# A quarter of the state products of layer 0 on ScalarE and TensorE, with new PSUM turns and slots

## The chip, the core and the metric

The kernel runs on one core of a Trainium2 chip. The metric is the device time of one launch in microseconds. The core has five engines that run side by side, each in the order of its own queue: TensorE (PE), VectorE (DVE), ScalarE (ACT), GpSimd (POOL) and SyncE (SP), which here issues the DMA transfers. They wait for each other through semaphores.

## The reference, cut to what matters

The program is a network of four layers on a tensor of 4 x 96 x 64 x 64. Only layer 0 is touched by the change. It is two Mamba blocks, each over sequences of 4096 steps:

```
xc    = silu(causal_conv4(h @ in_w[:, :192]) + conv_b)          # [L, 192]
dbl   = xc @ xproj_w                                             # 6 + 16 (B) + 16 (C) columns
delta = softplus(dbl[:, :6] @ dt_w + dt_b)                       # [L, 192]
dA    = exp(delta[..., None] * A)                                # [L, 192, 16]
dBx   = delta[..., None] * B[:, None, :] * xc[..., None]         # [L, 192, 16]
state[t] = dA[t] * state[t - 1] + dBx[t]                         # the scan over L
y     = sum over the 16 states of state * C, + Dp * xc
out   = seq + (y * silu(z)) @ out_w
```

After the two blocks come a pooled branch, a fusing product and a batch norm. All of it is float32.

## The kernel before, in words

Layer 0 is cut into 32 items: 4 sequences x 4 stretches of T = 1024 steps x 2 blocks. Within an item the 192 x 16 = 3072 pairs of channel and state are 24 tiles of 128 partitions x 1024 steps. A tile is (p, g, j): p one of three groups of 64 channels, j a half of it (32 channels), g one of four groups of 4 states. So a partition of a tile is one state of one channel.

A tile needs `da` = exp(delta * A), by ACT (line 488); `u` = (delta * xc) * B; the scan, by DVE (line 529); then, for the two tiles of one (p, g) together, a product with C by POOL (line 534, `times_c`) and a sum over the states by PE into `y` (line 551, `sum_y`). `delta` and `du` = delta * xc come in a layout of 64 channels by 2 x 512 steps; they are stored to DRAM (line 383) and read back with every channel on four partitions (`ddb`, `udb`, line 430). B and C rows go to DRAM as `cd` and come back spread over the partitions (`brep`, `crep`, line 416).

The product with B is made in two ways. For 14 tiles PE spreads the rows of B into a PSUM buffer with a 0/1 matrix (`rep`, line 474, two matmuls), and DVE multiplies (line 523), in place or into a second PSUM buffer. For 10 tiles, those with g = 3 and four with g = 2, POOL multiplies from SBUF (lines 509 and 511, `times_b`), and `da` is then put into PSUM by ACT (`dap`). There are two PSUM buffers of 128 x 1024 for this, tags `x` and `u`: `rep` always takes `x`, `dap` and the out-of-place product always `u`. Two more banks hold the tiles of the first stage (`ps`), two hold `y`.

The order of the work is written by hand. A loop over m = 24 k + t (line 613) gives to each engine's queue, for tile t of item k: the scan, the next `rep` or `dap`, the exp of the tile three ahead, a one-element product that puts the incoming state into `da` (line 497, `enter`), then POOL's products, sums, gates and projections at listed slots. The first stage of an item (norm, convolution, xproj, delta, z) is cut into steps, each at a slot; a slot below zero lies in the item before the one before. The slot order is fixed for PE, DVE, ACT and POOL; an engine runs what stands in its queue strictly in that order. SP's order is left to the scheduler, which follows the order of the program.

The names that the prediction uses: `center` (line 282, norm by a matmul, waits for the load of `x`), `nt` transposes (318), `n` copies (329), xc convolution (215, 16 matmul records a part), `join` (229, xproj), `dbl` copies (369), delta parts, Softplus (377), Silu (350), `start_y` (544), `sum_y` (551), gate (562), project (569 and 229), finish (581 to 591). `prepare` makes the weights before the first item; its `conv_taps` is the table of convolution taps, loaded to 97 partitions.

Of the kernel before, what the change touches and what calls it, by code (L numbers as in the profile page):

```python
# [20 lines left out]
T = 1024  # L21
# [29 lines left out]
class Net:  # L51
# [43 lines left out]
    def layer0(self, dram, scratch):  # L95
        tc, nc, ins = self.tc, self.nc, self.ins
        x_in = ins["x"]
        with ExitStack() as ctx:
# [3 lines left out]
            psum_y = ctx.enter_context(tc.tile_pool(name="l0y", bufs=2, space=PSUM))  # L102
# [44 lines left out]
            AHEAD = 3  # L147

            weights = {}

            def load_weights():
                for name, shape in (
                    ("sel_r", [128, 32]),
                    ("sel_b", [64, 4, 128]),
                    ("xproj", [128, 3, 2, 3 * 2 * NST + DTR]),
                    ("out_w", [128, 3, C]),
                    ("fus", [C, 2, C]),
                    ("gpw", [C, C]),
                ):
                    weights[name] = load(cp, name, shape)  # L160
                nc.sync.dma_start(dtw[C:], ins["dtw"])

            def prepare():
                with tc.tile_pool(name="l0s", bufs=1) as wk, tc.tile_pool(name="l0g", bufs=1) as sums_pool:
                    in_w = load(wk, "in_w", [C, 2, HID])
                    rows = wk.tile([C + 1, 2, 4, DIN], F32, name="conv_taps")
                    nc.sync.dma_start(rows, ins["conv_rows"].partition_broadcast(C + 1))
# [5 lines left out]
                    nc.vector.tensor_scalar_mul(nega, nega, -1.0)  # L173

# [14 lines left out]

                    layer(0)  # L190

                    for m in sorted(stages[0])[:4]:
                        for f in stages[0].pop(m):
                            f()
                    layer(1)
# [12 lines left out]
            both = [(at, slice(64 * q, 64 * q + 64)) for q, at in enumerate(halves)]  # L208

# [51 lines left out]
            def first_stage(k):  # L261
# [16 lines left out]
                @at_slot(-9)  # L278
                def _():
                    m["ps"] = [tile_ps(128), tile_ps(128)]  # L280
                    for q in range(8):
                        nc.tensor.matmul(
                            m["ps"][q // 4][:, q % 4 * C : q % 4 * C + C],
                            m["xn"][:, q * 128 : q * 128 + 128],
                            self.center,
                            start=True,
                            stop=True,
                        )

                @at_slot(-8)  # L290
                def _():
                    if k:
                        nt = wk.tile([128, 2, T + 1], F32, name="nt", tag="up2")[:, 0]
                    else:
                        nt = first_pool.tile([128, 8 * C], F32, name="nt")
                    m["nt"] = nt[:, : 8 * C].rearrange("p (q c) -> p q c", q=8)
                    m["rs"] = cp.tile([128, 8], F32, name="rs", tag="rs")
                    for q in range(8):
                        nc.scalar.activation(
                            m["nt"][:, q],  # L300
                            m["ps"][q // 4][:, q % 4 * C : q % 4 * C + C],
                            AF.Square,
                            accum_out=m["rs"][:, q : q + 1],
                        )
                    nc.scalar.activation(m["rs"], m["rs"], AF.Ln, scale=1.0 / C, bias=self.eps)
                    nc.scalar.activation(m["rs"], m["rs"], AF.Exp, scale=-0.5)

                @at_slot(-7)
                def _():
                    for q in range(8):  # L310
                        x = m["ps"][q // 4][:, q % 4 * C : q % 4 * C + C]
                        nc.scalar.mul(m["nt"][:, q], x, m["rs"][:, q : q + 1])
# [9 lines left out]
                @at_slot(-5)  # L322
# [23 lines left out]
                parts_of("xc", [(w_x[:, i, k], k) for k in range(4)], n, ((-4, -2), (-3, 0), (-1, 1)), 2)  # L346

                @at_slot(2)
# [12 lines left out]
                @at_slot(4)  # L361
# [4 lines left out]
                @at_slot(5)  # L366
# [6 lines left out]
                parts_of("delta", [(dtw[:, i], 0)], dbl, ((6, 7), (6, 7), (7, 8)), 1)  # L373

                @at_slot(9)
                def _():
                    nc.scalar.activation(m["delta"], m["delta"], AF.Softplus)
                    exp_set()
# [6 lines left out]
                @at_slot(10)  # L385
# [3 lines left out]
                @at_slot(11)  # L389
# [7 lines left out]
                parts_of("z", [(w_z[:, i], 3)], n, ((12, 13), (12, 13), (13, 14)), 2)  # L397

                for p in range(3):
                    for j in range(2):  # L400
                        at_slot((15, 23, 31)[p] + j)(lambda p=p, j=j: load_d(m, p, j))
                    at_slot((16 if k else 15, 23, 31)[p])(lambda p=p: load_u(m, p))
                for g, t in ((0, 21), (1, 24), (3, 25), (2, 27)):
                    at_slot(t)(lambda g=g: load_c(m, g))
                at_slot(17 if k else 6)(lambda: load_b(m, 3))
                at_slot(22)(lambda: load_b(m, 2))
# [40 lines left out]
            outer = [(0, 0), (0, 1), (3, 0), (1, 0), (1, 1), (3, 1), (2, 0), (2, 1)]  # L447
            inner = [(0, 0), (3, 0), (0, 1), (3, 1), (1, 0), (2, 0), (1, 1), (2, 1)]
            order = [(p, g, j) for p, eight in enumerate((outer, inner, outer)) for g, j in eight]
            pool_tiles = (2, 5, 7, 9, 11, 13, 15, 18, 21, 23)  # L450
            group_starts = (0, 3, 6, 8, 10, 12, 14, 16, 19, 22)
            ends = {max(t for t, x in enumerate(order) if x[:2] == (p, g)): (p, g) for p in range(3) for g in range(4)}
            sums = {5: (0, 0), 8: (0, 1), 9: (0, 3), 12: (0, 2), 14: (1, 0), 16: (1, 3)}
            sums |= {18: (1, 1), 19: (1, 2), 23: (2, 0), 24: (2, 1), 26: (2, 3), 27: (2, 2)}
            starts = {3: 0, 13: 1, 17: 2}
# [3 lines left out]

            def on_pool(m):  # L460
                return m % NTL in pool_tiles
# [5 lines left out]
            def rep(m):  # L467

                k, t = divmod(m, NTL)
                x = psum_x.tile([128, T], F32, name="rep", tag="x")  # L470

                for q, at in enumerate(halves):
                    rows = slice(32 * q, 32 * q + 32)
                    nc.tensor.matmul(  # L474
                        x[:, at], sel_b[rows, order[t][1]], made[k]["dbl"][rows, at], start=True, stop=True
                    )
                return x

            def exp(m):
# [3 lines left out]
                if on_pool(m):  # L483
                    da = psum_x.tile([128, T], F32, name="dap", tag="u")
# [5 lines left out]
            def enter(m):  # L490

                k, t = divmod(m, NTL)
                b, s, i = items[k]
                col = column(t)
                if s:
                    a0 = made[k]["da", t][:, :1]
                    nc.scalar.mul(a0, a0, state[:, b, i, col : col + 1])

# [3 lines left out]
            def times_b(k, p, g, js):  # L502

                u = made[k]["ud", p]
                up = wk.tile([128, 2, T + 1], F32, name=f"up{g}", tag=f"up{g}", bufs=g - 1)[:, :, :T]
                for j in js:
                    made[k]["up", p, g, j] = up[:, j]
                if len(js) == 2:
                    nc.gpsimd.tensor_mul(up, u, twice(made[k]["brep", g]))  # L509
                else:  # L510
                    nc.gpsimd.tensor_mul(up[:, js[0]], u[:, js[0]], made[k]["brep", g])  # L511

            def scan(m, x):
# [4 lines left out]
                if on_pool(m):  # L518
                    u = made[k].pop(("up", h, g, j))
                else:  # L520

                    u = x if on_pool(m + 1) else psum_x.tile([128, T], F32, name="u", tag="u")
                    nc.vector.tensor_mul(u, made[k]["ud", h][:, j], x)  # L523
                if ("hs", h, g) not in made[k]:
                    made[k]["hs", h, g] = wk.tile([128, 2, T + 1], F32, name="hs", tag="hs", bufs=5)
                hs = made[k]["hs", h, g][:, j]
                col = column(t)
                st = 0.0 if s == 0 else state[:, b, i, col : col + 1] if on_pool(m) else 1.0
# [13 lines left out]
            def start_y(k, p):  # L542
                y = made[k]["y", p] = psum_y.tile([128, MB], F32, name="y", tag="y")
# [54 lines left out]
            b_slots = {3: [(0, 1, 3, (0, 1))], 4: [(0, 0, 2, (1,))], 9: [(0, 1, 2, (0, 1))], 13: [(0, 2, 3, (0, 1))]}  # L598
            b_slots[20] = [(0, 2, 2, (1,)), (1, 0, 3, (0, 1))]
# [10 lines left out]
            with tc.manual_schedule(engines=engines):  # L610
                gp = global_pool()
                first = min(stages[0])
                for m in range(first, last + 19):
                    k, t = divmod(m, NTL)
                    if 0 <= m < last:
                        scan(m, x)
                    if m == -14:
                        x = rep(0)
                    if 0 < m + 1 < last:
                        if on_pool(m + 1):  # L620
                            exp(m + 1)
                        elif (t + 1) % NTL in group_starts:
                            x = rep(m + 1)
                    if 0 <= m + AHEAD < last and not on_pool(m + AHEAD):
                        exp(m + AHEAD)
                    if 0 <= m + AHEAD - 1 < last and not on_pool(m + AHEAD - 1):
                        enter(m + AHEAD - 1)
# [4 lines left out]
                    for ahead, *what in b_slots.get(t, ()):  # L632
                        if 0 <= k + ahead < len(items):
                            times_b(k + ahead, *what)
                    for k0 in range(max(k - 1, 0), min(k + 1, len(items))):
# [13 lines left out]
                        if at == 35:  # L649
# [751 lines left out]
def _constants():  # L1401
# [3 lines left out]
    sel_b = np.stack([(k[:64, None] % 32 == 4 * g + p[None] // 32) for g in range(4)], 1)  # L1405
# [48 lines left out]
def _lay_out(i):  # L1454
# [20 lines left out]
    for k, v in (("rd", np.diagonal(a["r"])), ("id", np.diagonal(a["i"])), ("rb", a["rb"]), ("ib", a["ib"])):  # L1475
# [17 lines left out]
        "conv_rows": m["conv_w"].transpose(0, 2, 1)[None],  # L1493
# [39 lines left out]
```

## Time and profile before

| | |
|---|---|
| three timed runs | 3830.7, 3847.7, 3848.1 us, median 3847.7 |
| profiled execution, its own time | 3837.7 us |
| its span | 3835.5 us |
| layer 0's scans | from 78.9 to 2527.7 us |
| busy over the span | PE 3238.0, DVE 3036.5, POOL 2836.6, ACT 2387.5 us |
| granted PE clock, mean | 0.857 |

A row of the groups names the source line, the engine and the operation, what it writes and reads with partitions x elements, the count, the busy time and the mean of one in ns, and then the idle time of the engine just before it with what ended it. A fp32 matmul shows as two records. In the order of time the first two columns are the start and the length in us. A number in square brackets is the idle time before the instruction, with what ended it.

### The profile page before, as it was taken

The page shows a single profiled execution, that of the slowest core. Times are in us where ns is not written, and L with a number is a line of the kernel's source. Part 1 is how long each engine was busy: PE and PEld are TensorE (multiplying, and loading weights), DVE is VectorE, ACT ScalarE, POOL GpSimd, SP SyncE. Part 2 cuts the span into 40 slices and gives each one's busy share as a digit, 9 for nine tenths or more (in the row PEclk, how much of TensorE's full clock was granted, in tenths as well). Part 3 has the DMA queues.
Part 4 walks back from the last instruction along what each step waited for, and adds up shares of the span by engine and source line. Part 5 has one row for each costly group of instructions (what it writes and reads, how often), then busy time and mean ns, then how long its engine had stood idle before and what let it go on. Part 6 is the DMA issues. An engine that isn't in the chain of part 4 may idle for free. (4 is left out here: it accounts for less than half of the span.)

```text
span 3835.5 us, 43134 instructions
## 1 busy us (share of the span) xinstructions
PE 3238.0 (84%) x13656; PEld 1305.1 (34%) x13656; DVE 3036.5 (79%) x2704; ACT 2387.5 (62%) x4640; POOL 2836.6 (74%) x922
## 2 busy tenths in 40 slices
PE   6888888888888888888888888756799998999888
PEld 2222222222222222222222222126544534766643
DVE  4999999999999899999999999962573384444649
ACT  4666676666667666776666666541345686656557
POOL 1999999999999999999999999932001064444527
PEclk9888888887888778887878778757899999999989
DMA  7656666666676566666666666556200000011101
GB/s 182 167 154 165 165 165 165 165 161 154 165 172 164 145 165 163 160 157 165 157 154 169 161 158 163 151 135 211 77 1 1 1 1 6 18 37 35 36 9 58
DMA packets 177867, 463.82 MB, mean 121 GB/s; under 512 B 50804, under 2 KB 52734, under 8 KB 174304
## 3 DMA queue, kind: packets, MB, share of 16 engines
q1 hardware_dynamic: 177640, 461.08, 47.3%
q8 instruction: 108, 1.77, 0.2%
q14 instruction: 119, 0.97, 0.1%
HBM read 387.40 MB, written 73.50 MB: 120 GB/s over the span
## 5 line engine op out<-in xcount | busy, mean ns | idle before, releaser
L534 POOL TENSOR_TENSOR hs<-hs,crep 128x2048 f32<-128x2048 f32 x384 | 1595.8, 4186 | 30.8 <-DVE hs L529 27.0
L474 PE MATMUL rep<-dbl,sel_b 32*128 32x512 f32 x1280 | 458.7, 794 | 365.6 <-DVE hs L529 364.4
L529 DVE TENSOR_TENSOR_SCAN hs<-da,rep 128x1024 f32<-128x1024 f32 x320 | 732.1, 2288 | 35.1 <-ACT da L488 0.7
L488 ACT ACTIVATE dap<-ddb,nega 128x1024 f32<-128x1024 f32 x320 | 356.9, 1115 | 491.8 <-DVE hs L529 490.9
L509 POOL TENSOR_TENSOR up<-udb,brep 128x2048 f32<-128x2048 f32 x128 | 580.3, 4533 | 84.0 <-DMA ddb<-dd 82.8
L488 ACT ACTIVATE da<-ddb,nega 128x1024 f32<-128x1024 f32 x448 | 512.4, 1144 | 76.6 <-DVE hs L529 71.9
L529 DVE TENSOR_TENSOR_SCAN hs<-dap,state,up 128x1024 f32<-128x1024 f32 x240 | 558.1, 2325 | 0.0
L551 PE MATMUL y<-hs,sel_r 128*32 128x512 f32 x3072 | 522.5, 768 | 16.8 <-POOL hs L534 16.7
L523 DVE TENSOR_TENSOR rep<-udb,rep 128x1024 f32<-128x1024 f32 x320 | 388.5, 1214 | 71.2 <-PE rep L474 71.1
L215 PE MATMUL ps<-n,w_x 97*64 97x512 f32 x1536 | 367.2, 621 | 0.0
L474 PEld LDWEIGHTS rep<-dbl,sel_b 32*128 32x128 f32 x1280 | 120.5, 218 | 672.9 <-issue 547.4
L529 DVE TENSOR_TENSOR_SCAN hs<-da,u 128x1024 f32<-128x1024 f32 x128 | 293.0, 2289 | 12.6 <-DVE u L523 0.5
L1091 POOL CAST hq<-y 128x1536 fp8e5<-128x1536 f16 x64 | 93.9, 1467 | 218.8 <-issue 122.6
L215 PEld LDWEIGHTS ps<-n,w_x 97*64 97x64 f32 x1536 | 110.6, 141 | 254.8 <-issue 196.7
L551 PEld LDWEIGHTS y<-hs,sel_r 128*32 128x32 f32 x3072 | 71.9, 122 | 359.9 <-issue 266.9
L529 DVE TENSOR_TENSOR_SCAN hs<-dap,up 128x1024 f32<-128x1024 f32 x80 | 181.3, 2266 | 1.8 <-ACT dap L488 1.7
L523 DVE TENSOR_TENSOR u<-udb,rep 128x1024 f32<-128x1024 f32 x128 | 157.4, 1229 | 25.4 <-DMA udb<-ud 11.9
L965 POOL MEMSET h<- 1x4096 f32 x1 | 3.5, 3506 | 212.9 <-DVE n L871 212.9
L1230 POOL TENSOR_TENSOR av<-av,ec 128x780 f32<-128x780 f32 x32 | 58.7, 1836 | 133.7 <-ACT av L1227 133.7
L511 POOL TENSOR_TENSOR up<-udb,brep 128x1024 f32<-128x1024 f32 x64 | 151.6, 2369 | 0.0
L544 PE MATMUL y<-xc,dp 128*128 128x512 f32 x192 | 140.6, 821 | 0.0
L1203 POOL TENSOR_TENSOR f<-p,p 128x390 f32<-128x390 f32 x64 | 65.1, 1038 | 95.0 <-DVE p L1195 95.0
(260 smaller groups left out, 5962.0 us busy)
## 6 DMA issues: line engine op xcount, KB each, us to landing
ddb<-dd SPq DMA_DIRECT2D x768, 128.0 KB
udb<-ud SPq DMA_DIRECT2D x768, 128.0 KB
crep<-cd SPq DMA_DIRECT2D x512, 128.0 KB
brep<-cd SPq DMA_DIRECT2D x256, 128.0 KB
dd<-delta SPq DMA_DIRECT2D x64, 384.0 KB
band<-in_band SPq DMA_DIRECT2D x24, 1024.0 KB
ud<-delta SPq DMA_DIRECT2D x62, 384.0 KB
x<-in_x SPq DMA_DIRECT2D x32, 384.0 KB
```

What stands on the lines that cost most here:

```text
L215: nc.tensor.matmul(ps[rows], w[:, 64 * p : 64 * p + 64], rhs[:, at.start + shift : at.stop + shift], start=k == 0, stop=k == len(ws) - 1, ...
L474: nc.tensor.matmul(x[:, at], sel_b[rows, order[t][1]], made[k]["dbl"][rows, at], start=True, stop=True)
L488: nc.scalar.activation(da, made[k]["dd", h, j], AF.Exp, scale=nega[:, col : col + 1])
L509: nc.gpsimd.tensor_mul(up, u, twice(made[k]["brep", g]))
L511: nc.gpsimd.tensor_mul(up[:, js[0]], u[:, js[0]], made[k]["brep", g])
L523: nc.vector.tensor_mul(u, made[k]["ud", h][:, j], x)
L529: nc.vector.tensor_tensor_scan(hs[:, 1:], made[k].pop(("da", t)), u, st, ALU.mult, ALU.add)
L534: nc.gpsimd.tensor_mul(hs[:, :, :T], hs[:, :, 1:], twice(made[k]["crep", g]))
L544: nc.tensor.matmul(y, dp[:, items[k][2], p], made[k]["xc"][:, p], start=True, stop=True)
L551: nc.tensor.matmul(made[k]["y", p][row : row + 32], sel_r, made[k]["hs", p, g][:, j, at], start=False, stop=True, skip_group_check=True,)
L1091: nc.gpsimd.tensor_copy(q, y2, saturate=False)
L1203: nc.gpsimd.tensor_add(f[i][:, r], pp[0][:, :, r, :], pp[1][:, :, 1 - r, :])
```

## The change

g = 3 becomes the ScalarE group (`GA`), g = 2 the POOL group (`GP`), g = 0 and 1 stay with DVE: 6, 6 and 12 tiles of an item.

For the ScalarE group the product is made with time on the partitions. PE transposes `dbl`'s 32 rows of B and C (8 transposes) into a `y` bank, and ACT keeps four columns of it as `bt`. PE transposes `du` (three parts, 4 transposes each) into a `y` bank, and ACT copies each to `udt`. ACT then writes `uta`, 32 instructions of 128 x 192 elements, each with one column of `bt` as its scale, over nine slots. When the tile comes, PE transposes 8 blocks of `uta` back into the PSUM buffer from which the scan reads `u`.

The two PSUM buffers now alternate by tile (`banks`), and the fills are listed by slot (`fills`). The tiles have a new order in each third. POOL makes six single products. The scan takes the incoming state as its pointer operand in every tile; `enter` is gone. `hs` has four named buffers in place of a ring of five, `nt` a buffer of its own, `y` two tags. Nearly all steps of the first stage, loads and sums have new slots. In `prepare` the convolution taps are loaded as one row and spread to 97 partitions by PE (three matmuls with K = 1) and DVE copies, in place of a broadcast DMA of 582 KB.

```diff
+            GP, GA = 2, 3
-                    ("sel_b", [64, 4, 128]),
+                    ("sel_b", [64, 2, 128]),
-                    rows = wk.tile([C + 1, 2, 4, DIN], F32, name="conv_taps")
-                    nc.sync.dma_start(rows, ins["conv_rows"].partition_broadcast(C + 1))
+                    row = load(wk, "conv_rows", [1, 2 * 4 * DIN])
...
+                    def spread_taps(q):
+                        at = slice(q * MB, (q + 1) * MB)
+                        ps = wide(C + 1, MB, q)
+                        nc.tensor.matmul(ps, one, row[:, at], start=True, stop=True)
+                        nc.vector.tensor_copy(taps[:, at], ps)
...
+            def y_bank(k):
+                return psum_y.tile([128, MB], F32, name="y", tag=f"y{k % 2}")
...
...
-                        nt = wk.tile([128, 2, T + 1], F32, name="nt", tag="up2")[:, 0]
+                        nt = wk.tile([128, 8 * C], F32, name="nt", tag="nt")
-                parts_of("xc", [(w_x[:, i, k], k) for k in range(4)], n, ((-4, -2), (-3, 0), (-1, 1)), 2)
+                parts_of("xc", [(w_x[:, i, k], k) for k in range(4)], n, ((-5, -4), (-3, -2), (-2, -1)), 2)
...
-                parts_of("delta", [(dtw[:, i], 0)], dbl, ((6, 7), (6, 7), (7, 8)), 1)
+                parts_of("delta", [(dtw[:, i], 0)], dbl, ((4, 4), (4, 4), (5, 5)), 1)
...
+                @at_slot(8)
+                def _():
+                    m["tb"] = y_bank(3 * k - 2)[:, : 8 * 2 * NST].rearrange("p (q s) -> p q s", q=8)
+                    for q in range(8):
+                        nc.tensor.transpose(
+                            m["tb"][:, q], dbl[: 2 * NST, q * 128 : q * 128 + 128], self.ident[: 2 * NST, : 2 * NST]
+                        )
+
+                @at_slot(9)
+                def _():
+                    m["bt"] = cp.tile([128, 8, 4], F32, name="bt", tag="bt", bufs=2)
+                    nc.scalar.copy(m["bt"], m["tb"][:, :, 4 * GA : 4 * GA + 4])
-                parts_of("z", [(w_z[:, i], 3)], n, ((12, 13), (12, 13), (13, 14)), 2)
+                parts_of("z", [(w_z[:, i], 3)], n, ((12, 12), (12, 12), (13, 13)), 2)
+                def turn_du(p):
+                    ps = m["ut", p] = y_bank(3 * k - 3)
+                    for a in range(4):
+                        at = slice(a * 128, a * 128 + 128)
+                        nc.tensor.transpose(ps[:, at], m["du"][:, p, at], self.ident)
+
+                def keep_du(p):
+                    if p == 0:
+                        m["udt"] = m["delta"].rearrange("t p (q c) -> t p q c", q=8)
+                    nc.scalar.copy(
+                        m["udt"][:, p].rearrange("t (h a) c -> t a h c", h=2),
+                        m.pop(("ut", p)).rearrange("t (a h c) -> t a h c", a=4, h=2),
+                    )
+
+                for p in range(3):
+                    at_slot(14 + p)(lambda p=p: (turn_du(p), keep_du(p)))
+
+                def weigh(of):
+                    if of[0] == 0:
+                        m["uta"] = wk.tile([128, 8, 6, 128], F32, name="uta", tag="uta")
+                    for e in of:
+                        q, s4 = divmod(e, 4)
+                        nc.scalar.mul(
+                            m["uta"][:, q, :, 32 * s4 : 32 * s4 + 32].rearrange("t (p j) d -> t p j d", p=3),
+                            m["udt"][:, :, q].rearrange("t p (j d) -> t p j d", j=2),
+                            m["bt"][:, q, s4 : s4 + 1],
+                        )
+
+                e = 0
+                for t, count in ((19, 4), (20, 3), (21, 4), (22, 3), (24, 3), (25, 4), (26, 2), (27, 3), (28, 6)):
+                    at_slot(t)(lambda of=range(e, e + count): weigh(of))
+                    e += count
...
+            d0, d1 = [(0, 0), (0, 1)], [(1, 0), (1, 1)]
+            p0, p1, a0, a1 = ([(g, j)] for g in (GP, GA) for j in range(2))
+            thirds = d0 + p0 + d1 + p1 + a0 + a1, d0 + p0 + a0 + d1 + p1 + a1, a0 + a1 + d0 + p0 + d1 + p1
+            order = [(p, g, j) for p, third in enumerate(thirds) for g, j in third]
+            fills = {2: 3, 5: 6, 6: 7, 7: 8, 10: 11, 11: 12, 14: 15, 15: 16, 16: 17, 17: 18, 20: 21, 23: 24}
...
+                if g == GA:
+                    for q in range(8):
+                        nc.tensor.transpose(x[:, q * 128 : q * 128 + 128], made[k]["uta"][:, q, 2 * h + j], self.ident)
+                    return
...
-                if len(js) == 2:
-                    nc.gpsimd.tensor_mul(up, u, twice(made[k]["brep", g]))
-                else:
-                    nc.gpsimd.tensor_mul(up[:, js[0]], u[:, js[0]], made[k]["brep", g])
+                up = made[k]["up", p, j] = wk.tile([128, T], F32, name="up", tag=f"up{j}")
+                nc.gpsimd.tensor_mul(up, made[k]["ud", p][:, j], made[k]["brep", GP])
...
-                st = 0.0 if s == 0 else state[:, b, i, col : col + 1] if on_pool(m) else 1.0
+                st = state[:, b, i, col : col + 1] if s else 0.0
...
+            b_slots = {1: (0, 0, 1), 3: (0, 1, 0), 9: (0, 1, 1), 11: (0, 2, 0), 20: (0, 2, 1), 23: (1, 0, 0)}
```

Steps of which only the slot number changes, left out above: `center` from -9 to -11, Square -8 to -10, `nt` products -7 to -9, `n` copies -5 to -6, Silu 2 to -1, the xproj join 4 to 3, `dbl` copies 5 to 3, Softplus 9 to 6, the store of `delta` 10 to 7, `du` and its store 11 to 9, `finish` 35 to 34. The load of `x` stays at -14.

## The prediction

> **What bounds the kernel now.** I first read the busy time by stretch, over layer 0 (75 to 2530 us; the rest of the kernel is not touched).
>
> ```profile
> core 0: us, PE busy (x) PEld busy (x) DVE busy (x) ACT busy (x) POOL busy (x), PEclk, DMA share, GB/s
> 75.00:2530.00 2455.00, 2067.51 (x8359) 597.67 (x8357) 2315.92 (x1312) 1624.06 (x3004) 2413.83 (x607) 0.82 0.64 159
> ```
>
> POOL is busy 98%, DVE 94%. The scans start at 78.9 us and the last ends at 2527.7: 32 items of 76.5 us. Next, the groups by form:
>
> ```profile
> L534 POOL TENSOR_TENSOR hs<-hs,crep 128x2048 f32<-128x2048 f32 x384 | 1595.8, 4186 | 30.8 <-DVE hs L529 27.0 <-PE y L551 3.7
> L529 DVE TENSOR_TENSOR_SCAN hs<-da,rep 128x1024 f32<-128x1024 f32 x320 | 732.1, 2288 | 35.1 <-ACT da L488 0.7 <-ACT dap L488 0.5 <-DVE rep L523 0.5
> L509 POOL TENSOR_TENSOR up<-udb,brep 128x2048 f32<-128x2048 f32 x128 | 580.3, 4533 | 84.0 <-DMA ddb<-dd 82.8 <-DMA crep<-cd 1.3
> L529 DVE TENSOR_TENSOR_SCAN hs<-dap,state,up 128x1024 f32<-128x1024 f32 x240 | 558.1, 2325 | 0.0
> ...
> L523 DVE TENSOR_TENSOR rep<-udb,rep 128x1024 f32<-128x1024 f32 x320 | 388.5, 1214 | 71.2 <-PE rep L474 71.1
> ...
> L394 POOL TENSOR_TENSOR delta<-delta,xc 128x1536 f32<-128x1536 f32 x31 | 106.7, 3441 | 0.0
> ...
> L312 ACT ACTIVATE nt<-ps,rs 128x96 f32<-128x96 f32 x248 | 60.3, 345 | 0.0
> ```
>
> Divided over an item, POOL has 12 x 4.186 + 4 x 4.533 + 2 x 2.369 (L511) + 3.441 = 76.5 us: exactly the period. POOL is the bound. The DVE pitches are in the order of time:
>
> ```profile
> 1424.79 2.33 DVE L529 TENSOR_TENSOR_SCAN hs<-dap,state,up 128x1024 f32<-128x1024 f32 x1
> 1427.20 1.23 DVE L523 TENSOR_TENSOR u<-udb,rep 128x1024 f32<-128x1024 f32 x1
> 1428.54 2.29 DVE L529 TENSOR_TENSOR_SCAN hs<-da,u 128x1024 f32<-128x1024 f32 x1
> 1430.74 1.21 DVE L523 TENSOR_TENSOR rep<-udb,rep 128x1024 f32<-128x1024 f32 x1
> 1432.05 2.29 DVE L529 TENSOR_TENSOR_SCAN hs<-da,rep 128x1024 f32<-128x1024 f32 x1
> ```
>
> A DVE tile takes 1.33 + 2.21 = 3.54 us, a POOL tile 2.24, or 2.42 where a product into a fresh buffer follows; a gate adds 0.58. 14 x 3.54 + 10 x 2.24 + 4 x 0.18 + 3 x 0.58 = 74.4 us, so DVE has 2.1 us to spare per item. Last, the waits of layer 0 and PE's order of time:
>
> ```profile
> ACT dap L488 <- DVE hs L529: 490.9, 205, 4.8
> PE rep L474 <- DVE hs L529: 364.4, 180, 6.3
> ```
>
> ```profile
> 1425.02 2.08 PE L474 MATMUL rep<-dbl,sel_b 32*128 32x512 f32 x4 [2.16 <-DVE hs L529]
> ...
> 1443.88 1.13 PE L474 MATMUL rep<-dbl,sel_b 32*128 32x512 f32 x4 [1.24 <-DVE hs L529]
> ```
>
> ACT and PE wait 15 and 11 us per item for a PSUM buffer: that is their reserve. The fill that follows a long wait takes 2.08 us, the other 1.13.
>
> [...]
>
> **The change, part by part, per item.**
> *POOL*: two B rows become one; 10 tiles' products become 6 single ones. 50.2 + 6 x 2.369 + 3.4 = 67.9 us: 8.6 less, no longer the bound.
> *DVE*: 12 own tiles, 6 POOL tiles, 6 ScalarE tiles. The state is now a pointer in every scan with s > 0. By form the same scan takes 2.325 with it and 2.266 without, so +0.06 on three quarters of the 12 DVE tiles' scans, 0.5 us; the 2.24 of the others holds it already. 12 x 3.54 + 12 x 2.24 + 6 x 0.18 + 1.74 + 0.5 = 72.7 us (the 0.18 falls before each of six pairs), 72.8 with `da` in SBUF for six of them (2.288 against 2.266). This is the new floor, 3.7 below the period.
> *ACT*: off, 14 one-element products on 3/4 of the items, 0.19 pitch: 2.0. On, 32 weighings of 192 elements: 0.19 + 0.16 = 0.35 each, 11.2 (bounds 0.32, L312's rate, and 0.45 with L312's unoverlapped 0.345: 10 to 14); three copies of `du` at 0.58, 1.7; `bt` 0.2. 417.8 us per 610 (the stretch from 690) is 52.4; it becomes 63.5. It fits in 73, but only in queue order.
> *PE*: off, 10 fills of 1.06 pitch; on, 6 of them, 48 transposes of `uta`, 12 of `du`, 8 of `dbl`. L318 gives 0.13 a transpose with 96 weights, L834 (128x128) 0.147: 7.1 + 1.7 + 0.8. Sum +5.4; 64.7 busy (515.5 us per 610) become 70.
> *Moved*: all first-stage steps 1 to 4 slots. Products into `delta` go from slot 11 to 9, so their two stores of 384 KB now stand ahead of the next `x` load in SP's queue, with the store of `xd` too; `center`, which needs that `x`, moves from slot 15 to 13. `hs` has four named buffers for five in a ring, `nt` one of its own.
> *Prologue*: DVE waits 23 us for `conv_taps` until 29.9 us. Three K=1 matmuls replace that load: some 15 us earlier at the first convolution. But in item 0 the weighings and the next item's convolutions and Silu now stand ahead of its second exp group on ACT, roughly 12 us. I count zero, bounds -12 to +8.
>
> **Where DVE will still wait**, from full-clock pitches (sum_y 0.99, xc 3.58, join 2.76, start_y 1.06, a ScalarE tile's fill 1.2):
> 1. From the fill at slot 17, PE has two sum_y, start_y and a third sum_y, transposes, then (after ACT's 1.2 us copies to `n`) xc, fill, sum_y, xc, sum_y, xc: some 20.1 us. Behind the last, ACT has copy 0.55, Silu and table loads 5.5, exp 1.05, three weighings 1.05, exp of the POOL tile 1.1: 9.3. Both, and scans 2 to 16 (43.6), make 73.0 plus handoffs: as long as DVE's floor itself. I take 0.7 lost before scan 2.
> 2. PE idles about 4 us in slots 0 to 2, so the fill, sum_y and part of join in slots 2 to 4 run at half clock; copies of `dbl`, next exp and the six last weighings follow. Join so ends some 2.5 us later; the six weighings end 0.6 late for the tile at slot 6.
> 3. `x`: `du` ends on POOL 18.5 us after scan 4 (three C products, one B, `du`); 1.57 MB at the 240 GB/s of a `ud` store (3.3 us of packets), plus 1.7 to start: 8.2. `center` 1.95 and the tile 15 fill 1.2 end at 29.9 of the 29.5 to 30 that DVE needs: 0.3. All fills of 15 to 18 queue behind `center`.
> 4. Turning `du` in slots 15 and 16 waits for ACT's copies of the one before (ACT has Square and `nt` work between); the fill of 18 stands behind it: 0.3.
> Sum 1.9, so 74.7 us per item: (76.5 - 74.7) x 32 = 58 us off. The profiled execution's own time is 3837.7 (span 3835.5): 3780. The three timed runs are 3831 to 3848, median 3848, 10 above it; I leave the level at the profile's, 3780.
>
> **Rivals.**
> *PE and ACT become the bound* (slower). 70 us of PE work, 4 idle in slots 0 to 2, 1 to 2 waiting for `x`, is already 75.5. If half clock holds where it now recovers, say through the transposes of slots 14 to 17 (three fills 0.9 longer each, fill of 18 0.85, center 1.7) and slots 5 to 7 (two more fills), DVE waits 6 rather than 1.9: 79 us, +80, 3918. It decides once the waits exceed 3.7 us per item. For it: the half clock in a third of layer 0, in-order queues. [...]
> *POOL's relief is eaten* (no change). Only `x` has to be 1.7 us later than worked out: 76.5 us, 3838.
> *Nearly the floor*. The new slots hide items 1 to 4: 73.3, 103 us off, 3735.
> That the change is inert is excluded: POOL's instruction count falls.
>
> **How the numbers follow.** Forecast 0.48 (own range 3755 to 3815), floor 0.14, no change 0.12, slower 0.26. A measurement of this kernel tells about 0.5% from nothing, 19 us: faster 0.62, same 0.12, slower 0.26. The range: the low end is the floor; the high end holds half of the slower case (78 us per item): 3735 to 3885. ACT's 0.45 bound (+3 us in ACT's chain) lies inside it.
>
> **What would show it.** POOL's busy share in layer 0 falls to about 90%, DVE's rises to 97%; 12 single B products less double ones per item; weighings at 0.35 pitch; waits of DVE on the fills below 2 us per item, found at tiles 2, 6, 15 and 18. Wrong if DVE waits above 3.7 us per item on the `uta` fills or on ACT's exp, if PE's clock drops below 0.8, or if ACT's weighings cost over 0.45.

## The result, and the profile after

The changed kernel takes 3934.6 us (median of four runs, 3931.4 to 3935.7), the kernel before 3845.6 us in the same comparison (3830.7 to 3848.1). The ratio is 1.024, with a 95% interval of 1.021 to 1.027. The change made the kernel slower by 89 us, where 58 us faster were forecast.

The profiled execution has a span of 3933.9 us, 98.4 more than before. The loss lies in layer 0, whose scans now run from 68.5 to 2628.6 us:

| | before | after | difference |
|---|---|---|---|
| first scan starts | 78.9 | 68.5 | -10.4 |
| item 0 | 76.8 | 85.6 | +8.9 |
| items 1 to 31, each | 76.52 | 79.82 | +3.30, together +102.4 |
| last scan ends | 2527.7 | 2628.6 | +100.9 |

First the busy time over layer 0, in the columns of the same view of before.

```profile
core 0: us, PE busy (x) PEld busy (x) DVE busy (x) ACT busy (x) POOL busy (x), PEclk, DMA share, GB/s
75.00:2620.00 2545.00, 2017.70 (x9936) 788.52 (x9932) 2255.13 (x1240) 1947.02 (x3793) 2131.56 (x603) 0.87 0.58 146
```

POOL has gone from 98% to 84%, DVE from 94% to 89%, ACT from 66% to 77%. No engine is full any more: POOL stopped being the bound, and nothing took its place as a busy engine. So the new time is made of waits. The mean clock granted to TensorE in layer 0 rose, from 0.82 to 0.87, so the average hides what is found below about single places. The groups by form of the changed kernel (instructions with the same line, tiles and shapes together), with the rows that answer to those of before and those of the new operations:

```profile
L600 POOL TENSOR_TENSOR hs<-hs,crep 128x2048 f32<-128x2048 f32 x384 | 1598.4, 4178 | 415.3 <-DVE hs L595 297.8
L595 DVE TENSOR_TENSOR_SCAN hs<-da,state,rep 128x1024 f32<-128x1024 f32 x288 | 669.6, 2340 | 116.7 <-PE rep L544 103.7
...
L571 POOL TENSOR_TENSOR up<-udb,brep 128x1024 f32<-128x1024 f32 x192 | 452.9, 2359 | 68.6 <-DMA udb<-ud 59.7
...
L451 ACT ACTIVATE uta<-delta,bt 128x192 f32<-128x192 f32 x1024 | 380.9, 443 | 0.0
...
L595 DVE TENSOR_TENSOR_SCAN hs<-da,rep 128x1024 f32<-128x1024 f32 x96 | 217.7, 2281 | 43.3 <-PE rep L544 39.8
```

The prices are near the forecast: six single B products of 2.359 us per item, the weighings (L451) at 0.443 us by the record of one and 0.37 of ScalarE's time for each (380.9 us for 1024, where 0.35 was forecast; an estimate from the pitches of the kernel before, 0.19 for one element and 1.05 for 1024, also gives 0.35 for 192), and a scan with the state as a pointer at 2.340 against 2.281 without, the +0.06 of the working. The last columns are what changed. POOL used to stand idle 31 us ahead of its C products, and now stands idle 415, most of it for the scans. The scans wait for `rep` filled at line 544, which is TensorE turning `uta` back into the scan's buffer. The waits of layer 0 say the same, and go one step further back (waited time in total, times, longest):

```profile
DVE hs L595 <- PE rep L544: 143.5, 56, 6.3
...
PE ps L299 <- DMA x<-xd: 58.5, 15, 4.4
PE ps L299 <- DMA x<-in_x: 50.9, 13, 4.9
```

In 28 of 31 items `center` (now line 299) waits for the load of `x`, 3.9 us each time: 109 us together. No such wait stood in the kernel before, where `center` comes two slots later and `x` stands ahead of the stores of `du` in SP's queue. Two lines of SP's queue before, 13 us apart:

```profile
1407.00 1.30 SPq L258 DMA_DIRECT2D x<-in_x  x1
...
1420.09 1.24 SPq L383 DMA_DIRECT2D ud<-delta  x2
```

To place the loss inside the item I took the distance from each scan's start to the next one's, by position in the item, as a mean over items 2 to 30, and set against it what the instructions between them take (2.26 for a bare scan, 3.54 with a DVE product, 0.58 more for a gate). The sum of the differences is 7.2 us, which with the floor of 72.8 gives the 80.0 of an item:

| scan waits before | predicted, us per item | measured |
|---|---|---|
| tile 15 (fill behind `center`, behind `x`) | 0.3 | 4.4 |
| tile 2 (exp behind the Silus) | 0.7 | 1.2 |
| tile 21 | none | 0.9 |
| tile 18 (turning of `du`) | 0.3 | 0.3 |
| tile 6 (weighings) | 0.6 | 0.25 |

One item in the order of time, changed kernel, start and length in us: the end of `du` on POOL, then SP's queue, then TensorE, then the scans on DVE.

```profile
1390.53 3.44 POOL L424 TENSOR_TENSOR delta<-delta,xc 128x1536 f32<-128x1536 f32 x1
```

```profile
1394.00 1.24 SPq L413 DMA_DIRECT2D ud<-delta  x2
1395.33 1.29 SPq L661 DMA_DIRECT2D scratch<-x  x1
1396.72 1.95 SPq L275 DMA_DIRECT2D x<-in_x  x1
1398.72 1.68 SPq L492 DMA_DIRECT2D ddb<-dd  x3
```

```profile
1404.12 3.69 PE L299 MATMUL ps<-center,x 96*128 96x96 f32 x16 [3.88 <-DMA x<-in_x]
1407.60 1.91 PE L544 MATMUL rep<-ident,uta 128*128 128x128 f32 x8
```

```profile
1402.49 2.34 DVE L595 TENSOR_TENSOR_SCAN hs<-dap,state,up 128x1024 f32<-128x1024 f32 x1
1409.55 6.82 DVE L595 TENSOR_TENSOR_SCAN hs<-da,state,rep 128x1024 f32<-128x1024 f32 x3 [4.72 <-PE rep L544]
```

`du` ends at 1393.97. SP can then issue two stores of `du` and one of the block's output, and only at 1396.72 the load of `x`, for which `center` waits until 1404.12, 10.1 us after `du` (10.3 on the mean over 29 items). TensorE has stood still for 3.9 us by then, and does `center` and the fill for tile 15 at half the clock: 3.69 us (3.48 to the start of the fill) and 1.91, where the experiments below show 1.9 to 2.0 and 1.04. The scan of tile 15 starts 4.7 us late, and everything after it in the item is late with it. The busy time by stretch, in the columns from above, has the granted clock of TensorE from 1404 to 1408 us at 0.52:

```profile
1394.00:1404.10 10.10, 5.61 (x30) 1.14 (x23) 9.83 (x7) 6.34 (x10) 8.38 (x3) 1.00 0.87 212
1404.00:1408.00 4.00, 3.88 (x18) 3.91 (x19) 0.83 (x1) 0.00 (x0) 4.00 (x2) 0.52 1.00 239
```

The trace shows both halves of this. The load of `x` is used 7.4 us after its issue at 1396.72, and the two stores of `du` move ahead of it: their 384 packets of 2 KB (786 KB) start from 1395.23 us on, 98% of them by 1398.87, and packets of 4 KB, among which those of `x` are, start from 1398.31 on. The wait for `x` is 3.9 us on the mean, and the half clock follows: in the 27 items with a wait of 3.2 to 4.9 us `center` took 2.9 to 3.7 us and the fill after it 1.85 to 1.92. But it followed shorter waits too: in two items of this kernel TensorE waited 1.63 and 1.24 us ahead of `center`, and the fill behind it still took 1.91; in the kernel before, the fill that the prediction shows at 2.08 us had waited 2.16. So the length of one wait does not decide it here, and the last section has what the traces show in its place.

### The profile page after: what moved, and what is told of

Its sections match the earlier page's. It is cut to its first block, busy times and chain, and to the rows that moved or that the text cites. A ratio compares the mean times of both kernels' runs of the same rounds, so it can differ in the third digit from the quotient of the medians.

```text
span 3933.9 us, 46826 instructions
## 1 busy us (share of the span) xinstructions
PE 3209.7 (82%) x15326; PEld 1508.4 (38%) x15326; DVE 2993.5 (76%) x2644; ACT 2722.3 (69%) x5456; POOL 2567.5 (65%) x922
## 5 line engine op out<-in xcount | busy, mean ns | idle before, releaser
L595 DVE TENSOR_TENSOR_SCAN hs<-da,state,rep 128x1024 f32<-128x1024 f32 x288 | 669.6, 2340 | 116.7 <-PE rep L544 103.7
L571 POOL TENSOR_TENSOR up<-udb,brep 128x1024 f32<-128x1024 f32 x192 | 452.9, 2359 | 68.6 <-DMA udb<-ud 59.7
L549 PE MATMUL rep<-dbl,sel_b 32*128 32x512 f32 x768 | 252.7, 737 | 168.5 <-DVE hs L595 167.8
L451 ACT ACTIVATE uta<-delta,bt 128x192 f32<-128x192 f32 x1024 | 380.9, 443 | 0.0
L595 DVE TENSOR_TENSOR_SCAN hs<-dap,state,up 128x1024 f32<-128x1024 f32 x144 | 335.9, 2332 | 27.7 <-ACT dap L560 23.7
L595 DVE TENSOR_TENSOR_SCAN hs<-da,state,u 128x1024 f32<-128x1024 f32 x144 | 338.1, 2348 | 18.9 <-PE y L617 3.6
L544 PE MATMUL rep<-ident,uta 128*128 128x128 f32 x1536 | 257.4, 318 | 80.4 <-DVE hs L595 63.0
L544 PEld LDWEIGHTS rep<-ident,uta 128*128 128x128 f32 x1536 | 212.6, 167 | 176.7 <-issue 102.4
L595 DVE TENSOR_TENSOR_SCAN hs<-da,rep 128x1024 f32<-128x1024 f32 x96 | 217.7, 2281 | 43.3 <-PE rep L544 39.8
L586 DVE TENSOR_TENSOR rep<-udb,rep 128x1024 f32<-128x1024 f32 x192 | 232.3, 1210 | 0.0
```

What stands on the lines that cost most here:

```text
L451: nc.scalar.mul(m["uta"][:, q, :, 32 * s4 : 32 * s4 + 32].rearrange("t (p j) d -> t p j d", p=3), m["udt"][:, :, q].rearrange("t p (j d) - ...
L544: nc.tensor.transpose(x[:, q * 128 : q * 128 + 128], made[k]["uta"][:, q, 2 * h + j], self.ident)
L549: nc.tensor.matmul(x[:, at], sel_b[rows, g], made[k]["dbl"][rows, at], start=True, stop=True)
L571: nc.gpsimd.tensor_mul(up, made[k]["ud", p][:, j], made[k]["brep", GP])
L595: nc.vector.tensor_tensor_scan(hs[:, 1:], made[k].pop(("da", t)), u, st, ALU.mult, ALU.add)
```

## The experiments

My theory after this comparison: the late load of `x` and the half clock that follows its wait are the whole of the slowdown, and ScalarE's added work is not. The rival is the one that the prediction names: TensorE and ScalarE as a chain are the bound, so that a wait taken away at tile 15 comes back elsewhere.

### The load of `x` two slots earlier

```diff
-                @at_slot(-14)
+                @at_slot(-16)
                 def _():
                     m["xn"] = load_x(b, s, i) if k else x0
```

> The changed kernel with one edit: the load of x of the item after next is issued at slot 8 in place of slot 10, so that it stands ahead of the two stores of du and of the store of xd or scratch in SP's queue. Theory A (the load of x behind those stores holds center, center holds the fill of tile 15 in PE's queue, and DVE stands there 4.4 us an item): the wait before the scan of tile 15 falls from 4.4 to about 0.3 us, PE does center at full clock (1.95 in place of 3.5 us), the item goes from 80.0 to about 75.8 us, and the kernel from 3934 to about 3800. Theory B (PE and ACT are full, whatever x does): the wait moves to the tiles behind (18, 21 and 2), the item stays above 78.5 us, and the kernel above 3885.

Measured: 3781.6 us (3781.3 to 3785.0), ratio to before 0.986 (0.983 to 0.989). One number in the source takes some 150 us off the changed kernel and makes it faster than the one before. Items take 75.05 us. SP's queue, TensorE and DVE in this kernel, at the same place in the item:

```profile
1378.53 0.42 SPq L275 DMA_DIRECT2D x<-in_x  x1
1382.28 1.24 SPq L413 DMA_DIRECT2D ud<-delta  x2
1383.61 1.30 SPq L661 DMA_DIRECT2D xd<-x  x1
```

```profile
1388.45 1.13 PE L299 MATMUL ps<-center,x 96*128 96x96 f32 x8
1390.12 1.13 PE L299 MATMUL ps<-center,x 96*128 96x96 f32 x8 [0.53 <-ACT z L356]
1391.08 1.04 PE L544 MATMUL rep<-ident,uta 128*128 128x128 f32 x8
```

```profile
1393.63 6.80 DVE L595 TENSOR_TENSOR_SCAN hs<-da,state,rep 128x1024 f32<-128x1024 f32 x3
```

`x` is issued before `du`'s stores, no `center` waits for it, and the fill behind `center` runs at full clock in every item (1.04). The distance from tile 14's scan to tile 15's falls from 6.63 to 2.31 us, near the 2.26 of a bare scan. The waits before tiles 18 and 21 fall with it, from 0.3 and 0.9 to 0.1 and 0.2: they came in the main from the late `center`. DVE is busy 95% of the time from 690 to 1300 us, against 89% in the changed kernel. What remains of the waits is 1.1 us at tile 2, 0.4 at tile 6, and small ones.

### `center` two slots later, the load left where it is

This asks whether it is the order on the queue or the distance from load to use that counts. `center` then also stands behind the fills of tiles 15 and 16 in TensorE's queue. The three steps are `center`, Square and the `nt` products.

```diff
-                @at_slot(-11)
+                @at_slot(-9)
...
-                @at_slot(-10)
+                @at_slot(-8)
...
-                @at_slot(-9)
+                @at_slot(-7)
```

> The changed kernel with the load of x left where it is, behind du's stores and the scratch store, but the matmuls of center, the squares and the scaling of the norm two slots later (slots 15, 16 and 17 of 24 instead of 13, 14 and 15), where the kernel before has its center. Theory A (what matters is the distance between x's landing and center, not where x stands on the queue): center no longer waits for x, tile 15's scan loses its wait of 4.4 us, and the time comes near to the run with x first, 3780 to 3800 us (0.986 to 0.991), if the rest of the norm still ends before the transposes at slot 18. Rival B (the norm's scaling and du's turning and copies now crowd ScalarE and TensorE in slots 16 and 17, so tile 18's or 21's fill is late instead): over 3840 us (above 1.001).

Measured: 3797.9 us (3790.1 to 3805.2), ratio 0.990 (0.987 to 0.993). Theory A holds: `x` is as late on the queue as in the changed kernel (issued 2.8 us after `du` ends), but `center` finds it there, and tile 15's scan waits for nothing (2.24). TensorE fills the gap with fills and turns of `du`, and `center` runs at full clock, here without a wait before it:

```profile
1479.16 1.92 PE L299 MATMUL ps<-center,x 96*128 96x96 f32 x16
```

The price that B named is there too, only smaller: the norm's later products reach the convolutions, and the scan of tile 21 waits 1.0 us, as its fill stands behind a convolution that began late. Items take 75.3 us. Either remedy is enough: the fault is the two together, an `x` issued behind the stores and a `center` moved forward to meet it.

### TensorE kept busy ahead of `center`

The load is left late. Six spare matmuls into the buffer of `center` fill its wait; what is computed stays the same.

```diff
                     m["ps"] = [tile_ps(128), tile_ps(128)]
+                    for _ in range(3 if k > 1 else 0):
+                        for at, rows in both:
+                            nc.tensor.matmul(
+                                m["ps"][0][rows],
+                                w_z[:, i, :64],
+                                n[:, at.start + 3 : at.stop + 3],
+                                start=True,
+                                stop=True,
+                                skip_group_check=True,
+                            )
                     for q in range(8):
```

> The changed kernel, with x as late as it is, but PE does three pairs of spare matmuls (about 3 us at full clock, into the bank that center overwrites) while it waits for x, in every item from the third. It computes the same. Theory A has two parts, the wait itself and the half clock that follows it: center then takes 1.95 in place of 3.5 us and the fill of tile 15 takes 1.1 in place of 1.9, so some 2.2 of the 4.4 us go, the item is near 77.8 us and the kernel near 3865. If the clock plays no part, the time stays at 3934 within 10.

Measured: 3899.6 us (two runs, 3892.2 and 3907.1), ratio 1.017 (1.013 to 1.021). The gain is 35 us, half of what was expected. In the order of time, TensorE of this kernel (line numbers 10 higher from `center` on):

```profile
1374.44 2.74 PE L300 MATMUL ps<-n,w_z 97*64 97x512 f32 x12
1378.43 2.02 PE L309 MATMUL ps<-center,x 96*128 96x96 f32 x16 [1.25 <-DMA x<-in_x]
1380.29 1.04 PE L554 MATMUL rep<-ident,uta 128*128 128x128 f32 x8
```

In this item the half clock is gone: `center` takes 2.02 instead of 3.69, the fill 1.04 instead of 1.91, and `x` comes 10.1 us after `du` as before (`du` ends at 1368.33). But the spare matmuls did not do this everywhere. In 11 of the 29 items 1 to 29 the fill still took 1.8 to 1.9 us, as in this one:

```profile
2005.23 2.64 PE L309 MATMUL ps<-center,x 96*128 96x96 f32 x16 [1.53 <-DMA x<-in_x]
2007.66 1.92 PE L554 MATMUL rep<-ident,uta 128*128 128x128 f32 x8
```

TensorE's wait for `x` was the same in both kinds, 1.4 us on the mean. The distance from scan 14 to 15 is 5.66 us in these 11 items and 4.77 in the other 18; over the same 29 items of the changed kernel it is 6.85. So the half clock is worth about 2.1 us where it is gone. On the mean over the 29 items 1.7 us are gained, where 2.2 were expected; the two runs differ by 15 us, so the rest of the shortfall stays open. What is left in those, 2.5 us above the bare scan of 2.26, is `x` itself, late at full clock too.

### Most of ScalarE's weighings left out

From the second item on 26 of the 32 weighings aren't done, and the buffer of item 0 is used again; the six last ones stay, so that the tile's fill still waits for ScalarE in its place.

```diff
                     if of[0] == 0:
-                        m["uta"] = wk.tile([128, 8, 6, 128], F32, name="uta", tag="uta")
+                        if k == 0:
+                            made[0]["kept"] = wk.tile([128, 8, 6, 128], F32, name="uta", tag="uta")
+                        m["uta"] = made[0]["kept"]
                     for e in of:
+                        if k and e < 26:
+                            continue
```

> The changed kernel without the first 26 of 32 weighings on ACT from the second item on (the tile of weighed products is then that of the first item, so a part of the computation is left out); the last six stay, and with them the order of waits. ACT has 9.7 us less an item. Theory A (ACT is not the bound; only the exp of tile 2, behind Silu, and the fill of tile 6 are late by it): about 1.4 us an item go, 3890. Theory B (ACT is full): DVE comes near its own 73 us, under 3750.

Measured: 3913.9 us (two runs, 3913.6 and 3914.2), ratio 1.020 (1.017 to 1.024). Theory A holds in kind, but only half of its 1.4 us per item came. The weighings left out are 26/32 of L451's 380.9 us, 9.7 us per item by the records, and the time falls by 21 us in all, 0.7 us per item. Tile 15's scan still waits 3.7 us, since nothing about `x` has changed. Tile 2's wait is gone (its distance is 2.45 instead of 3.48), but 0.4 us each have come up at tiles 5 and 6. Were ScalarE's load the bound, 9.7 us less of it could not have brought only 0.7. This half of the rival is out as the cause of the slowdown; TensorE's load was not taken away in any run, but with `x` first the same load of both engines fits in 75.05 us.

### The convolution taps alone

The kernel before, with only the change in `prepare`: the taps loaded as one row and spread by TensorE.

```diff
-                    rows = wk.tile([C + 1, 2, 4, DIN], F32, name="conv_taps")
-                    nc.sync.dma_start(rows, ins["conv_rows"].partition_broadcast(C + 1))
+                    row = load(wk, "conv_rows", [1, 2 * 4 * DIN])
...
+                    spread_taps(0)
+                    spread_taps(1)
...
+                    spread_taps(2)
```

> The kernel before with one part of the change alone: the convolution taps come as one row and are spread by PE and DVE. Theory: the first scan starts about 15 us earlier than 78.9, since ACT's new work isn't there, and nothing behind it changes: 3838 - 15 = 3823, ratio 0.996. Rival (the first scan is held by the 16 loads for the pooled sums or by the loads of weights): under 5 us.

Measured: 3816.7 us (eight runs, 3814.3 to 3822.4), ratio 0.996 (0.994 to 0.997). The first scan starts at 65.5 us, 13.4 earlier than before, and the rest of the kernel is unchanged (items of 76.6 us). The theory holds, and the rival with its loads is out. This part of the change is worth some 0.4% by itself; in the changed kernel item 0 gives most of it back (85.6 us instead of 76.8).

### The three weighings ahead of tile 2's exponential, moved later and moved earlier

With `x` first, the largest wait left is 1.1 us at tile 2, whose exponential stands on ScalarE behind two Silus, a table load (1.28 us in the trace of that run), the exponential of tile 1 and three weighings. Both of these kernels have the load of `x` two slots earlier.

```diff
-                for t, count in ((19, 4), (20, 3), (21, 4), (22, 3), (24, 3), (25, 4), (26, 2), (27, 3), (28, 6)):
+                for t, count in ((19, 4), (20, 3), (21, 4), (22, 3), (25, 4), (26, 4), (27, 4), (28, 6)):
```

> The changed kernel with two edits: the load of x two slots earlier, as in the run with x first (3781.6 us, 75.05 us per item), and the three weighings of the slot of the first tile moved to the last slots, so that tile 2's exponential no longer stands behind them after the Silus. Theory A (tile 2's wait of 1.1 us per item is ScalarE's queue: Silus, table load, three weighings at 0.35 to 0.44 us, then the exponential): the exponential comes about 1.05 us earlier, the wait nearly goes, 74.0 us per item, 3748 us (0.977 of before). Rival B (the wait moves on: tile 6's fill, now 0.6 us late, is late by as much more): 75.0 us per item, 3780 us (0.986).

Measured: 3792.2 us (3778.0 to 3795.4), ratio 0.987 (0.983 to 0.991). Rival B holds. Tile 2's distance falls from 3.40 to 2.39, so the wait is gone. Tile 5's rises from 2.30 to 2.99, tile 6's from 3.23 to 3.49. Of the 1.0 us gained 0.95 is lost at once, and the time doesn't differ from that with `x` first.

The same three weighings can also go to earlier slots, where ScalarE stands idle:

```diff
-                for t, count in ((19, 4), (20, 3), (21, 4), (22, 3), (24, 3), (25, 4), (26, 2), (27, 3), (28, 6)):
+                for t, count in ((19, 4), (20, 3), (21, 6), (22, 4), (25, 4), (26, 2), (27, 3), (28, 6)):
```

> The changed kernel with the load of x two slots earlier and the three weighings that stood ahead of tile 2's exponential moved to earlier slots (two to slot 21, one to slot 22), where ScalarE stands idle for 1.1 and 1.5 us, instead of to later ones. Theory A (tile 5's late fill in the run with later weighings came from the weighings themselves ending later, so with them moved the other way both waits of tiles 2 and 5 go): 74.0 us per item, about 3748 us (0.977 of before). Rival B (the scans that start 1 us earlier meet TensorE's chain behind the Silus, whose length from the last copy of xc to delta's fills is fixed, so tile 5's or 6's fill is late by what tile 2 gained): 75 us per item, about 3780 us (0.986).

Measured: 3779.4 us (3772.0 to 3780.9), ratio 0.984 (0.980 to 0.989). Rival B again: tile 2 is free (2.38), tiles 5 and 6 wait as in the run before (2.93 and 3.49), items take 74.9 us. ScalarE and DVE of this kernel in the order of time show why:

```profile
1429.68 1.07 ACT L386 COPY dbl<-ps 102x512 f32<-102x512 f32 x2 [3.14 <-PE ps L246]
1430.64 1.13 ACT L560 ACTIVATE dap<-ddb,nega 128x1024 f32<-128x1024 f32 x1
```

```profile
1431.87 2.35 DVE L595 TENSOR_TENSOR_SCAN hs<-dap,state,up 128x1024 f32<-128x1024 f32 x1 [0.97 <-ACT dap L560]
1434.14 0.67 DVE L628 TENSOR_TENSOR z<-y,z 128x512 f32<-128x512 f32 x1
1435.42 4.80 DVE L595 TENSOR_TENSOR_SCAN hs<-da,state,rep 128x1024 f32<-128x1024 f32 x2 [0.61 <-PE rep L544]
```

ScalarE is idle for 3.1 us here, because the copies of `dbl` wait for the join on TensorE, and tile 5's exponential stands behind those copies. The exponential can't move up without passing them in the queue. A DVE that isn't held up at tile 2 only comes to this chain sooner. So in this stretch (Silu, join, `dbl`, exponential) the order of ScalarE and TensorE is the limit for both placements of the weighings; no run changed that order. This is the fastest of the versions by its median, 56 us under the kernel before that ran beside it (3835.2); from the run with `x` first the measurement doesn't tell it apart.

## Why the prediction was wrong

The prediction failed at step 3 of "Where DVE will still wait", the load of `x` and what follows it, and at nothing else that is large. Its working there was: `du` ends on POOL 18.5 us after scan 4, `x` takes 8.2, `center` 1.95, the fill 1.2, together 29.9 where DVE needs 29.5 to 30. Measured in the item shown, from the end of scan 4 (1375.5, its start at 1373.15 plus 2.35): `du` 18.5, `x` 10.1, `center` 3.5, fill 1.9, together 34.0.

- *`x` 10.1 instead of 8.2.* The working gave the whole of the DMA engines to the 1.57 MB of `du`, output and `x`. The trace has 2.14 MB moved in these 10.1 us (212 GB/s, in the row for 1394 to 1404.1 us above). The difference of 0.57 MB is more than `x` and what lay ahead of it: reads of `delta` (`ddb`) issued at 1398.72, right behind `x`, moved in the same 10.1 us. At the 240 GB/s of the working that would be 2.4 us, about the excess of 1.9; this is an estimate, and no run isolates this part. Of the 1.7 us that the working put ahead of the transfer 1.26 are in the trace, from the end of `du` to the first packet at 1395.23.
- *`center` 3.5 instead of 1.95 and the fill 1.9 instead of 1.2: 2.2 us together.* This is the half clock. The prediction knew it (it shows a fill at 2.08 us beside one at 1.13, and the "PE and ACT" rival has it), but it summed step 3 from full-clock pitches. The kernel before spoke against that already: there `center` took 3.73 us in 21 of 31 items, while POOL was the bound. With `x` first, and with `center` later, no fill behind `center` runs at half clock in any item; the run with spare matmuls puts the worth of the half clock at some 2.1 us.
- *Tile 21, 0.9 us that no step had.* It is late by the same cause: with `x` first it falls to 0.2.

The line of `center` in the kernel before, right behind the fill at 2.08 us that the prediction shows:

```profile
1427.02 3.73 PE L282 MATMUL ps<-center,x 96*128 96x96 f32 x16
```

The rest of the sum held. POOL, DVE and ScalarE came out near their prices. TensorE came out lower: 63.3 us of an item (2017.7 of 2545 us in the row above) where 70 were counted, with its clock up from 0.82 to 0.87. The prologue was counted as zero and is -10.4 + 8.9 = -1.5 us; the taps alone start the first scan 13.4 us earlier. Step 1 (tile 2) was 0.7 and is 1.2, step 2 (tile 6) 0.6 and is 0.25 (the half clock it counted on is in the trace: behind a wait of 4.25 us that ends at 1444.87 the fill took 2.08, the sum behind it 1.94 and the join 4.39 us), step 4 (tile 18) 0.3 and is 0.3. With step 3's fault taken out by moving one load, the kernel takes 3781.6 us, with 2.2 us of waits per item where 1.9 were counted: the forecast describes this kernel, not the one that was asked about. That the time falls within 2 us of 3780 is in part chance, since the kernel before took 3832.1 us beside it and not 3837.7: 50 us were gained where 58 were forecast. Of the signs of being wrong that the prediction lists, the first one came (4.5 us of waits for the `uta` fills per item); the clock in layer 0 stayed above 0.8, and the weighings below 0.45.

Of the rivals, the one named "POOL's relief is eaten" had the right place: `x` only 1.7 us later than worked out. It was 1.9 later. But it stopped at 76.5 us per item and 3838 us, for it too left out the half clock. The slower rival had the right size (79 us per item, 3918) by the wrong route: it put the half clock into the transposes of slots 14 to 17 with TensorE's and ScalarE's work as the bound. Its price for `center`, 1.7 us, and one of its three fills are what happened, but what set them off was a transfer.

The error in method is plain. Step 3 had a margin of less than half a microsecond between 29.9 and 29.5 to 30, was the sum of four terms, and two of them take 1.8 times as long at TensorE's half clock (3.5 for 1.95, 1.91 for 1.04). Such a step deserves its own case, with a probability of its own and with the matmuls at half clock, rather than the 0.3 us of its mean.

## What to carry over

When a change moves a consumer forward, check the producer's place on its DMA queue as well: the load kept its slot, but the stores of another step were moved ahead of it, and nothing in the load's own lines changed. Where TensorE waits for a transfer, price the matmuls behind the wait at half clock too, and look in the old trace how often they ran so there: here `center` and the fill took 3.5 and 1.9 us, where 1.95 and 1.2 were counted. And a wait taken away in front of an in-order chain can come back at the next point where that chain is met, as two of the experiments showed (1.0 us gone at tile 2, 0.9 us come up at tiles 5 and 6).

## What was not expected of the hardware

A `uta` fill of eight 128 x 128 fp32 transposes ran at 1.04 to 1.09 us amid other work, with no sign that transposes themselves lower the clock; the mean granted clock in the kernel with `x` first is 0.909, above the 0.857 of the kernel before, though it has 48 more transposes per item for the fills alone. What the rival feared of transposes did not show here.

The half clock came without a long idle time as well as with one. By the traces' own record of the granted clock, it went from full to half 102 times in layer 0 of the kernel before. In none of these had TensorE been without a matmul for the whole 4 us ahead; in the median it had been busy for 46% of them, where it is busy for 84% of layer 0, and its longest idle time in them was 2.2 us. A wait of 3.9 us or more, as long as the mean wait for `x`, reached into these 4 us in 7 of the 102 cases. In the changed kernel it went down 75 times, again with 46% in the median against 79% over layer 0, and such a wait was there in 33. So in these kernels little work over some microseconds, and not one long wait alone, stood ahead of the half clock; from which share on it comes was not measured.

And a load of 384 KB took 7.4 us from its issue to its use at 1404.12 in the changed kernel, with the DMA engines busy 98% and more in each 2 us from 1396 us on.
